# Small-number chains of a graph attention moved to GpSimd, its row work held behind the pairs, and its sums centred by the product that turns them

## The chip, the core and the metric

The kernel runs on one core of a Trainium2 chip. The core has five engines that work side by side: TensorE (PE) for matrix products, VectorE (DVE) and ScalarE (ACT) for elementwise work, GpSimd (POOL)[...], and SyncE (SP), which here only issues loads. Each engine runs its own instructions in a fixed order and waits for others at semaphores. Data lies in SBUF (128 partitions); matrix products land in PSUM[...]. The metric is the device time of one execution in microseconds (us), lower is better.

## The reference

Four layers of a graph network act on 4096 nodes of 64 features, with one dense 4096 x 4096 matrix of 0/1 edges `adj`. Each ends in a residual sum and a LayerNorm.

```python
x = _layernorm(x + _L0_gnn_ref(x, adj, L0_gnn_W, L0_gnn_b))     # mean over neighbours, linear, relu
x = _layernorm(x + _L1_gnn_ref(x, adj, L1_gnn_r, ...))          # hyperbolic attention
x = _layernorm(x + _L2_gnn_ref(x, adj, L2_gnn_weight, ...))     # weights that decay along the neighbours
x = _layernorm(x + _L3_gnn_ref(x, adj, L3_gnn_att_w, ...))      # hyperbolic attention
```

The change concerns the two attentions, which compute the same thing with small differences:

```python
adj_att = jax.nn.sigmoid(left[:, None] + right[None, :] + b_att[0]) * adj   # 4096 x 4096
x_local = logmap(x[:, None, :], x[None, :, :], c)                           # 4096 x 4096 x 64
support_t = jnp.einsum('ij,ijd->id', adj_att, x_local)
return proj(expmap(x, support_t, c), c)
```

The pairwise part (first three lines) is the large one. What follows, `expmap` and `proj` with the residual sum and the LayerNorm, works row by row: for each node a few dot products over its 64 features, then some eighty operations on single numbers (square roots, a tanh, quotients), and at the end the new row as a combination of the old row and `support_t`.

## The kernel before

Nodes are cut into 32 blocks of 128 and, as the receiving side, into four groups of 1024 (eight blocks each; `GROUPS`, taken from the last to the first; this text numbers them 0 to 3 in the order in which they run). The four layers follow each other: layer 0 (stage 0), the first attention (stage 1), the decaying layer (stage 2), the second attention (stage 3). The array `place` holds the stage and a counter of places in it.

**Pairs.** In an attention, `attend` (L914) goes over the 32 source blocks of a group, two at a time: 16 pairs per group. For each block PE forms `z` (128 x 1024, six products: L935, L938, L941), ACT makes the sigmoid (L943) and a square (L946), DVE joins z with the sigmoid (L949). Then DVE finishes both blocks at once (L951, inputs `sq` and `t`, both in SBUF), and PE adds them up in `acc` (L955). At the end of a group ACT copies `acc` to `sums` (L962), features along the partitions.

**Row work.** `move` (L972) is what follows the sums of a group: four transposes bring them to rows (`to_rows_of`, L969), ACT copies them to SBUF (L985), DVE takes the sum over the features (L988), subtracts the mean (L991); POOL multiplies by x (L992), ACT squares (L994), DVE reduces both (`uu` L997, `d` L999). Then comes the chain of small numbers on DVE, each instruction on 128 x 8 elements (one number per node): L1001 to L1065, with three reciprocal square roots of ten instructions each (`rsqrt`, L673 to L679: an integer seed and three Newton steps), a tanh on ACT (L1020) and a reciprocal (L1036). At the end POOL multiplies x by `p` (L1067), DVE multiplies u by `q` (L1068) and adds both (L1071). `norm_rows`, `prepare`, `linear` and `spread_left` are other row work: they make the next layer's inputs.

**What sets the order.** Row work is written as generators. `tick` (L592) is called between the pairs; at each place it lets the generators of two queues go one step, and `yield n` asks for n places until the next. `later` puts a generator into one of the queues; a queue works off one generator after the other. `after`, `soon` and `near` choose the n. But these places only set the order in which the program is written: in the attentions a scheduler of the framework orders each engine's instructions by its own estimate of what is ready, so that an instruction of row work can be issued earlier or later than where it was written (in stages 0 and 2 PE and ACT are held in the written order). At the end of each group `attention` (L1266) queues `move` of that group and, from the second group on, what turns the previous group's result into the next layer's input (`behind`: `linear` in the first attention, the output DMA in the second). Both go into the first queue, except in the last group.

## Time and profile before

| | us |
|---|---|
| median of 3 runs (1148.69 to 1153.72) | 1151.56 |
| the profiled execution | 1150.32 |
| its span (first to last instruction) | 1148.8 |
| layer 0 until the first pair of the first attention | 192.23 |
| first attention, first to last pair | 192.23 to 535.98 |
| second attention, first to last pair | 779.12 to 1111.37 |
| last pair to the last row operation | 1111.37 to 1142.82 |
| one L949 / L951 on DVE (mean) | 1.216 / 2.289 |
| one small instruction on DVE (128 x 8) | 0.16 |
| one large row operation on DVE (128 x 512) | 0.68 |
| one large product on POOL (L992, 128 x 512) | 1.28 |

The profile comes from one execution. Its busy column gives each engine's busy time; a row of the groups tells line, engine, operation, tiles, count, busy time and mean duration. An instruction's duration includes a part in which the next one already runs: on DVE, starts of neighbours are about 0.08 us closer than the durations suggest. Of an attention's groups each has a first L949 and a last L951; the time between them is what the group takes. An idle time carries the name of the engine that ended it.

### The profile page before, as it was taken

How to read it: one execution, taken by the hardware profiler on the slowest of the kernel's cores; microseconds unless marked ns; L12 is line 12 of the kernel's file. 1: busy time of each engine (PE TensorE's matmuls, PEld its weight loads, DVE VectorE, ACT ScalarE, POOL GpSimd, SP SyncE). 2: the span in 40 equal slices, each digit the busy share in tenths (PEclk: the TensorE clock that was granted, in tenths of full speed). 3: DMA queues.
4: the chain of work that ended last, by engine and by line, in shares of the span. 5: the costliest groups of instructions: out<-in, count | busy, mean ns of one | idle time of the engine just before them, and what ended most of it. 6: DMA issues, size and time to landing. Idle time of an engine off the chain costs nothing.

```text
span 1148.8 us, 13484 instructions
## 1 busy us (share of the span) xinstructions
PE 1012.6 (88%) x4832; PEld 386.9 (34%) x4917; DVE 964.3 (84%) x1901; ACT 820.6 (71%) x886; POOL 60.3 (5%) x97
## 2 busy tenths in 40 slices
PE   6999897899899999988999987898898999999870
PEld 3445544233333333332333232233333333233320
DVE  5687898999999899989773476529998999999996
ACT  0003215899889788976767778888998998889850
POOL 0020120000000000000000020000000000000001
PEclk9999998999999999999999999899999999999995
DMA  9999998556566466644988976686465666566400
GB/s 344 421 381 400 373 417 329 193 176 218 176 210 218 164 209 210 220 169 140 323 297 312 341 268 235 220 278 235 150 217 183 220 218 204 204 210 206 149 1 21
DMA packets 38418, 271.57 MB, mean 236 GB/s; under 512 B 4550, under 2 KB 4550, under 8 KB 5574
## 3 DMA queue, kind: packets, MB, share of 16 engines
q1 hardware_dynamic: 37440, 269.50, 65.3%
q10 hardware_dynamic: 902, 1.12, 0.3%
q8 instruction: 40, 0.66, 0.2%
q14 instruction: 36, 0.29, 0.1%
HBM read 269.55 MB, written 1.05 MB: 236 GB/s over the span
## 4 chain that ended last, share of the span: by engine, by line
DVE 57%; PE 26%; ACT 7%; DMA 4%; issue 3%; POOL 2%; SPq 0%; ACTq 0%; POOLq 0%
DVE t L951 20%; DVE t L949 20%; PE z L1372 8%; PE acc L1387 5%; PE acc L955 4%; DMA edges<-in_adj_dram 4%; PE acc L1229 3%; DVE junk L741 2%; ACT sq L946 2%; ACT sq L1381 2%; PE z L935 1%; PE z L938 1%; POOL sq L768 1%; PE aux L842 1%; PE z L941 1%
## 5 line engine op out<-in xcount | busy, mean ns | idle before, releaser
L943 ACT ACTIVATE sig<-left_b,right 128x1024 f32<-128x1024 f32 x256 | 293.8, 1149 | 45.9 <-DVE t L949 35.0
L949 DVE SCALAR_TENSOR_TENSOR t<-z,sig 128x1024 f32<-128x1024 f32 x256 | 309.9, 1216 | 13.9 <-ACT sq L946 12.9
L946 ACT ACTIVATE sq<-z,turn 128x1024 f32<-128x1024 f32 x256 | 281.5, 1106 | 27.3 <-PE z L941 25.1
L951 DVE SCALAR_TENSOR_TENSOR t<-sq,t 128x2048 f32<-128x2048 f32 x128 | 292.9, 2289 | 0.7
L955 PE MATMUL acc<-t,xe 128*64 128x512 f32 x1024 | 260.2, 619 | 32.3 <-DVE t L951 28.7
L935 PE MATMUL z<-edges,two_i 128*128 128x512 bf16 x465 | 183.1, 394 | 19.7 <-DVE t L949 19.5
L938 PE MATMUL z<-lo_hi,hi_lo 128*128 128x512 f16 x512 | 194.1, 379 | 3.2
L941 PE MATMUL z<-dst,src 74*128 74x512 f16 x512 | 195.1, 381 | 0.0
L1381 ACT ACTIVATE sq<-z,at_edge 128x512 bf16<-128x512 f32 (+1 forms) x192 | 152.6, 829 | 51.3 <-PE z L1372 47.9
L955 PEld LDWEIGHTS acc<-t,xe 128*64 128x64 f32 x1024 | 64.0, 138 | 168.5 <-DVE t L951 88.4
L741 DVE SCALAR_TENSOR_TENSOR t<-edges 128x2048 bf16<-128x2048 f32 x32 | 73.9, 2311 | 38.5 <-DMA edges<-in_adj_dram 37.5
L1372 PE MATMUL z<-edges,pass_by 128*128 128x512 bf16 x241 | 87.5, 400 | 17.3 <-ACT sq L1381 15.8
L935 PEld LDWEIGHTS <-two_i 128*128 128x128 bf16 x512 | 50.3, 98 | 142.7 <-issue 97.7
L1229 PE MATMUL acc<-edges,first 128*128 128x512 bf16 x241 | 77.4, 397 | 21.4 <-DMA edges<-in_adj_dram 20.7
L1387 PE MATMUL acc<-sq,halves 128*64 128x512 bf16 x512 | 82.0, 398 | 5.7 <-ACT sq L1381 3.5
L1372 PE MATMUL z<-edges,enter 128*128 128x512 bf16 x240 | 85.1, 397 | 0.1
L1229 PE MATMUL acc<-edges,third 128*65 128x512 bf16 x256 | 80.9, 398 | 0.6
L741 DVE SCALAR_TENSOR_TENSOR junk<-edges 128x2048 bf16<-128x2048 f32 x32 | 73.2, 2286 | 5.1 <-DMA edges<-in_adj_dram 4.8
L938 PEld LDWEIGHTS <-hi_lo 128*128 128x128 f16 x512 | 50.3, 98 | 67.9 <-issue 23.7
L941 PEld LDWEIGHTS <-src 74*128 74x128 f16 x512 | 49.4, 96 | 69.2 <-issue 4.0
L1229 PEld LDWEIGHTS <-first 128*128 128x128 bf16 x256 | 24.3, 98 | 50.2 <-issue 22.6
L1387 PEld LDWEIGHTS <-halves 128*64 128x64 f16 x512 | 18.9, 108 | 63.0 <-issue 62.7
(260 smaller groups left out, 758.3 us busy)
## 6 DMA issues: line engine op xcount, KB each, us to landing
edges<-in_adj_dram SPq DMA_DIRECT2D x256, 1024.0 KB, 4.9
x<-in_x_dram SPq DMA_DIRECT2D x4, 256.0 KB
out_dram<-x ACTq DMA_DIRECT2D x4, 256.0 KB, 4.0
w_sb<-in_L_gnn_W_dram ACTq DMA_DIRECT2D x1, 32.0 KB, 4.8
given<-in_L_gnn_b_dram ACTq DMA_DIRECT2D x1, 0.2 KB
given<-in_L_gnn_bias_dram ACTq DMA_DIRECT2D x1, 0.2 KB
given<-in_L_gnn_b_att_dram ACTq DMA_DIRECT2D x1, 0.0 KB
given<-in_L_gnn_att_b_dram ACTq DMA_DIRECT2D x1, 0.0 KB
```

The lines of the kernel that those rows point to most:

```text
L741: V.scalar_tensor_tensor(junk, a, 0.0, a, ALU.not_equal, ALU.not_equal, accum_out=odd[:, n : n + 1])
L935: nc.tensor.matmul(half, two_i, edge[:, at : at + W], start=True, stop=False)
L938: nc.tensor.matmul(half, hi_lo[:, of], lo_hi[:, to], start=False, stop=False)
L941: nc.tensor.matmul(half, src[:, of], dst[:, to], start=False, stop=True)
L943: nc.scalar.activation(sig, left_b, AF.Sigmoid, bias=right[:, j : j + 1])
L946: nc.scalar.activation(sq[:, k], zp, AF.Square, bias=turn, scale=-1.0 / UNIT)
L949: V.scalar_tensor_tensor(t[:, k], zp, 0.0, sig, ALU.max, ALU.mult)
L951: V.scalar_tensor_tensor(t, sq, HIGH**2, t, ALU.add, ALU.mult)
L955: nc.tensor.matmul(acc[h * D : (h + 1) * D, :], xe[:, j, :], t[:, k, h * W : (h + 1) * W], start=j == BLOCKS[0], stop=j == BLOCKS[-1],)
L1229: nc.tensor.matmul(accs[h][:m], lhs[:, j, :], edge[:, at : at + W], start=j == BLOCKS[0], stop=j == BLOCKS[-1],)
L1372: nc.tensor.matmul(z[:, h : h + W], lhs, rhs[:, h : h + W], start=j == BLOCKS[0], stop=True, skip_group_check=True,)
L1381: nc.scalar.activation(w, z[:, :n], AF.Exp, bias=at_edge, scale=-LN2)
```

## The change

It has five parts.

1. A class `Small` carries the chain of small numbers in `move`. For all groups of an attention but the last it issues them on POOL, for the last on DVE as before. On POOL a fused operation (two in one) becomes two instructions (`stt`). The three integer seeds of the reciprocal square roots and the one reciprocal stay on DVE. The last three large operations also go to POOL (L1067, L1068, L1071 of before).
2. `pool_done` gives the number of places that the writing order leaves for POOL's work before an instruction of another engine that needs it.
3. The four transposes of `sums` become four products with a constant `centre` (128 x 130), which give the rows with their mean taken off and, as a 65th column, their sum. They come in two parts, each with its own ACT copy; L988, L989 and L991 go.
4. The reciprocal of `un` (L1018) becomes two small operations on the reciprocal square root, with two constants from `curved`.
5. `mark` records, at each place, the last instruction of the pairs on PE, ACT and DVE, and ties every row instruction of these engines that is issued there behind it in the engine's order (without a semaphore). This holds in groups 1 to 3 of an attention. The work `behind` now goes to the second queue in all groups, after nine places.

```diff
+            ROW_ENGINES = FIXED | {mybir.EngineType.DVE}
...
+            def mark(rows):
+                traced = nc.cur_bb.bb.instructions
+                for i in traced[seen[0] :]:
+                    if i.engine not in ROW_ENGINES:
+                        continue
+                    if not rows:
+                        pairs_last[i.engine] = i
+                    elif anchored[0] and i.engine in pairs_last:
+                        tc.add_manual_dep(
+                            i, pairs_last[i.engine].name,
+                            mybir.DependencyInfo(
+                                mybir.DependencyClass.NoSync, mybir.DependencyReason.DATA
+                            ),
+                            reason="row work behind the pairs",
+                        )
+                seen[0] = len(traced)
...
             def tick(n):
                 for _ in range(n):
                     place[1] += 1
+                    mark(False)
                     for queue in queues:
...
+                    mark(True)
...
+            def pool_done(small, large=0):
+
+                return 2 + int(small * 0.2 + large * 0.9)
...
+            class Small:
+                def __init__(self, on_pool):
+                    self.on_pool = on_pool
+                    eng = nc.gpsimd if on_pool else V
...
+                def stt(self, out, in0, scalar, in1, op0, op1):
+                    if not self.on_pool:
+                        V.scalar_tensor_tensor(out, in0, scalar, in1, op0, op1)
+                        return
+                    t = nums("pool_t")
+                    nc.gpsimd.tensor_scalar(t, in0, scalar, None, op0)
+                    nc.gpsimd.tensor_tensor(out, t, in1, op1)
+
+                def wait(self, small, large=0):
+
+                    return pool_done(small, large) if self.on_pool else soon()
+
+                def rsqrt(self, a, name, small):
+
+                    r, t = nums(name), nums("rs_t")
+                    if self.on_pool:
+                        yield self.wait(small)
+                    V.tensor_scalar(
+                        r.bitcast(I32), a.bitcast(I32), -0.5, float(0x5F3759DF),
+                        ALU.mult, ALU.add,
+                    )
+                    for _ in range(3):
+                        self.mul(t, r, r)
+                        if self.on_pool:
+                            self.mul(t, t, a)
+                            self.ts(t, t, -0.5, 1.5, ALU.mult, ALU.add)
+                            self.mul(r, t, r)
+                        else:
+                            self.stt(t, t, -0.5, a, ALU.mult, ALU.mult)
+                            self.stt(r, t, 1.5, r, ALU.add, ALU.mult)
+                    return r
...
+            centre = keep.tile([P, 2, D + 1], F32, name="centre")
+            V.memset(centre, 0.0)
+            for h in range(2):
+                of = slice(h * D, (h + 1) * D)
+                V.tensor_scalar(
+                    centre[of, h, :D], ident[of, of], -1.0 / D, None, ALU.add
+                )
+                V.memset(centre[of, h, D:], 1.0)
...
-                t = to_rows_of(sums)
-                yield near()
-                nc.scalar.copy(of.rearrange("p (h k) f -> p h k f", h=2), t)
-                held.pop()
-                yield near()
-                V.tensor_reduce(sum_1, of, AX.X, ALU.add)
-                V.tensor_scalar(k, sum_1, 1.0 / D, None, ALU.mult)
-                yield soon()
-                V.tensor_sub(u, of, over(k))
+                all_u = row.tile([P, WB, D + 1], F32, name="u_1")
+                u, sum_1 = all_u[:, :, :D], all_u[:, :, D]
+                for part in range(2):
+                    yield from free()
+                    t = take(F32, P, 2, 2, D + 1)
+                    for i in range(2):
+                        cols = slice((2 * part + i) * P, (2 * part + i + 1) * P)
+                        nc.tensor.matmul(t[:, i], sums[:, cols], centre, start=True, stop=True)
+                    yield near()
+                    nc.scalar.copy(
+                        all_u.rearrange("p (h k) f -> p k h f", h=2)[:, 2 * part : 2 * part + 2], t
+                    )
+                    held.pop()
+                    yield near()
                 nc.gpsimd.tensor_mul(w, xg, u)
-                yield after(12)
                 nc.scalar.activation(sq, u, AF.Square)
...
+                G = Small(s != GROUPS[-1])
+                yield G.wait(0, 1) if G.on_pool else near()
                 V.tensor_reduce(uu, sq, AX.X, ALU.add)
                 yield soon()
                 V.tensor_reduce(d, w, AX.X, ALU.add)
                 yield soon()
-                V.scalar_tensor_tensor(k, d, c2, sum_1, ALU.mult, ALU.add)
-                V.tensor_mul(k, k, rb[:, at])
+                yield soon()
+                G.stt(k, d, c2, sum_1, ALU.mult, ALU.add)
+                G.mul(k, k, rb[:, at])
...
-                V.reciprocal(r_un, un)
-                yield after(29)
+                G.ts(r_un, r, by_root, 1.0 / fac, ALU.mult, ALU.mult)
+                G.ts(r_un, r_un, by_short, None, ALU.min)
+                yield pool_done(19) if G.on_pool else after(29)
                 nc.scalar.activation(th, un, AF.Tanh, scale=lam)
...
+                if G.on_pool:
+                    yield G.wait(14)
                 V.reciprocal(den, den)
...
+                E = nc.gpsimd if G.on_pool else V
                 nc.gpsimd.tensor_mul(w, xg, over(p))
-                V.tensor_mul(u, u, over(q))
+                E.tensor_mul(u, u, over(q))
                 yield soon()
                 yield soon()
-                V.tensor_add(x_of(layer + 1)[:, at, :], u, w)
-                yield after(72)
+                E.tensor_add(x_of(layer + 1)[:, at, :], u, w)
+                yield pool_done(15, 3) if G.on_pool else after(72)
...
                     if n:
-                        last = n + 1 == NW
-                        later(in_turn((layer + 1, s + 1), behind(s + 1)), last, 9 * last)
+                        later(in_turn((layer + 1, s + 1), behind(s + 1)), True, 9)
                     later(move_s)
```

## The prediction

> **What bounds the kernel now.** I read the page's busy times and slices first, then the busy time by stretch, one stretch per attention group (a group is 1024 rows: 16 pairs of blocks).
>
> ```profile
> PE 1012.6 (88%) x4832; PEld 386.9 (34%) x4917; DVE 964.3 (84%) x1901; ACT 820.6 (71%) x886; POOL 60.3 (5%) x97
> ...
> DVE  5687898999999899989773476529998999999996
> ```
>
> DVE is at nine tenths through both attentions (slices 7 to 18 and 27 to 38), POOL is free. By group:
>
> ```profile
> core 0: us, PE busy (x) PEld busy (x) DVE busy (x) ACT busy (x) POOL busy (x), PEclk, DMA share, GB/s
> 192.23:278.98 86.75, 78.49 (x354) 28.31 (x359) 83.90 (x117) 79.08 (x78) 3.17 (x8) 0.97 0.56 194
> 278.98:361.91 82.93, 77.61 (x327) 26.77 (x332) 79.83 (x112) 72.75 (x70) 1.28 (x1) 0.98 0.60 203
> 362.13:448.62 86.49, 81.38 (x351) 29.20 (x354) 81.55 (x117) 74.37 (x75) 2.32 (x2) 1.00 0.57 195
> 448.69:535.98 87.29, 79.56 (x342) 28.24 (x348) 83.03 (x111) 73.25 (x71) 2.31 (x2) 0.99 0.57 193
> ...
> 865.93:948.93 83.00, 77.69 (x327) 26.77 (x332) 79.83 (x112) 72.75 (x70) 1.27 (x1) 0.98 0.59 203
> 949.16:1031.52 82.36, 77.40 (x327) 26.59 (x330) 80.93 (x118) 72.31 (x71) 2.32 (x2) 0.98 0.61 208
> 1031.52:1111.37 79.85, 72.43 (x308) 24.76 (x314) 79.85 (x109) 68.23 (x64) 2.32 (x2) 1.00 0.40 135
> ```
>
> The first row is group 0 of the first attention, then come groups 1 to 3 of each attention. Only these six can change; between their first and last instructions they take 257.0 + 245.4 = 502.4 us. Is DVE their bound? DVE's timeline (start, duration, engine, line) in the late pairs of group 0, which have no row work:
>
> ```profile
> 248.24 2.29 DVE L951 SCALAR_TENSOR_TENSOR t<-sq,t 128x2048 f32<-128x2048 f32 x1
> 250.54 2.55 DVE L949 SCALAR_TENSOR_TENSOR t<-z,sig 128x1024 f32<-128x1024 f32 x2
> 253.12 2.29 DVE L951 SCALAR_TENSOR_TENSOR t<-sq,t 128x2048 f32<-128x2048 f32 x1
> ...
> 257.74 2.29 DVE L951 SCALAR_TENSOR_TENSOR t<-sq,t 128x2048 f32<-128x2048 f32 x1
> ```
>
> From 248.24 to 257.74 two pairs take 9.50, so 4.75 each. Late in the second attention one small instruction stands in every gap:
>
> ```profile
> 1090.10 2.29 DVE L951 SCALAR_TENSOR_TENSOR t<-sq,t 128x2048 f32<-128x2048 f32 x1
> 1092.31 0.17 DVE L1009 TENSOR_SCALAR t<-t 128x8 f32<-128x8 f32 x1
> ...
> 1094.84 2.29 DVE L951 SCALAR_TENSOR_TENSOR t<-sq,t 128x2048 f32<-128x2048 f32 x1
> ```
>
> Again 4.74. A small instruction costs about 0.075 (next start after 1092.31: 1092.38), so three fill the 0.25 that DVE has spare per pair, and cost nothing. PE alone needs 4.53 of a pair (1.87 for `acc`, twelve products at 0.222), so 16 x 4.74 = 75.8 us is a group's floor here. The six groups are 47.4 us above it. That is large row work and stalls: in group 1, the pair with both sums and the wait for POOL takes 9.00, and 1.7 follows two pairs later because PE, having idled 1.74 and 1.31 us, runs its next products at half speed:
>
> ```profile
> 292.90 3.53 PE L955 MATMUL acc<-t,xe 128*64 128x512 f32 x8 [1.31 <-DVE t L951]
> ```
>
> against 1.94 elsewhere. Last, the tail: 31.45 us from the last L951 (1111.37) to the last add (1142.82), nearly all a DVE chain. The previous group's row work is still half undone there and goes first; the last group's begins only here:
>
> ```profile
> 1124.26 0.69 DVE L991 TENSOR_TENSOR u<-z,k 128x512 f32<-128x512 f32 x1
> 1126.40 0.69 DVE L999 TENSOR_REDUCE d<-w_att 128x8 f32<-128x512 f32 x1 [1.44 <-POOL w_att L992]
> ```
>
> **What the skill says.** "SBUF — State Buffer", Who interferes with whom: a VectorE instruction with two SBUF inputs and a GpSimd one that reads SBUF exclude each other for a whole instruction, whoever came first; with one SBUF input there is no conflict. The trace agrees, both ways. The timeline at 666 us:
>
> ```profile
> 666.07 2.28 DVE L741 SCALAR_TENSOR_TENSOR t<-edges 128x2048 bf16<-128x2048 f32 x1
> 666.22 2.22 POOL L806 COPY ys<-hl 128x16 f16<-128x16 f16 x1 [0.26 <-DVE hl L803]
> ```
>
> L806 takes 0.22 beside L949 (at 227.78), which reads PSUM and one SBUF tile, but 2.22 here. The other way, L795 took 1.54 instead of 0.68 behind POOL's L768. "GPSIMD Engine Reference", 3.1 Elementwise: about 2.6 cycles per element at 1.2 GHz for two inputs against VectorE's 1, and a dispatch in software; L992 (512 elements) took 1.28, so all but about 0.17 is elements. "TensorE: Matmul & The Clock Gate", Part 1: idle windows of some 3.4 us halve the clock; the 3.53 above fits.
>
> **Part 1: chains to POOL.** 94 POOL instructions per move: 90 small, four large. DVE keeps two reductions and four small ones (three seeds, one reciprocal). The built program places them at: uu and d in pair 2, seed before L951 of pair 4, reciprocal at the head of pair 8, seeds before L951 of pair 9 and at the head of pair 12. Gone from a group are 72 small DVE instructions (mostly hidden, so about nothing), sum_1, u, u x q and the add (four of about 0.60), and the 1.4 wait for POOL.
>
> The new cost: each of the four waits for a POOL chain, and DVE stands with all the pairs behind it. No row shows a dependent small POOL operation. Lower bound: 0.13 to 0.16, the spacing of independent copies (227.78, 227.91, 228.05, 228.21). Upper: 0.22 to 0.25 for one, plus DVE's release of POOL (0.08), with a mean of 0.43 for L811 beside DVE work as the extreme. I take 0.28 per dependent and 0.15 per free step. POOL has only the two L949 of a pair, some 2.3 us, since L951 shuts it out. First stretch, 11 steps in two windows: no wait. Pair 4 to tanh, 15 steps (14 dependent): 4.1 in two windows of 4.6, just in time. After tanh 11 dependent + 3 free = 3.5 in one window: 1.2 left over, done behind L951, so the reciprocal waits 1.3. To pair 9: 3.4 in 4.6, free. To pair 12: 18 x 0.28 + 3 x 0.15 = 5.5 in 4.6: waits 1.0. Sum 2.3 per group; a wait can't be below nothing, so quick steps bring at most these 2.3 back. L951 meeting a POOL instruction in flight waits too: up to 0.25 for small ones, inside DVE's spare 0.25; for the three large at the end (1.04, 1.04, 1.28) I take 0.5.
>
> **Part 2: centring by a product.** Per move four products with 130 columns in place of four transposes, two ACT copies of 260 columns (0.37 each, estimated from 0.58 for 512) in place of one of 512. What stays at the group's head: two reductions 1.2 less DVE's spare 0.25, and ACT's 0.57 + 0.74 + 0.62 = 1.9, which in the kernel before hid under DVE's 4.3; I take 1.8 in all.
>
> **Part 3: order.** `mark` adds no semaphore; it keeps row work of DVE, PE and ACT from going ahead of the pairs. In groups 2 and 3 of the first attention `linear` now lies spread over pairs 4 to 6 of the second queue: ACT 2 x (0.57 + 0.38), DVE 2 x 0.42, PE waiting for ACT's copies; I take 2.5. The `left_b` copies are spread over pairs 12 to 14: nothing, as in group 0 (pair 10, no longer than others). Output DMAs on ACT's queue come at pair 4 of the next group; the last at pair 15 of group 3 waits for POOL's add, which I expect in pair 14. `centre` and the constants are built during the first layer, whose DVE has gaps: nothing.
>
> **Tail.** With the previous move done, the last one starts when acc is ready (1114.71): copy 0.57, products 1.0, second copy 0.4, POOL 1.28, so d starts near 1118.2 instead of 1126.4. From there the same 16.4 chain (last group: still DVE). Gain 8.2.
>
> **Sum.** A group: 75.8 + 1.8 + 0.5 + 2.3 + 0.2 = 80.6; with `linear` 83.1. First attention 80.6 + 2 x 83.1 = 246.8 against 257.0: gain 10.2. Second 3 x 80.6 = 241.8 against 245.4: 3.6. Tail 8.2. Sum 22.0. The profiled execution, 1150.3 (span 1148.8), becomes 1128.3; the median shown, 1151.6, lies 1.2 above it, so 1129.5.
>
> **Rivals.** *DVE is the bound*, by its busy column: 72 x 0.075 + 2.4 + 1.4 = 9.2 per group, six times, and the tail: 63 off, 1088. Against it stands 4.75 in pairs without row work; the floor allows 47.4 + 8.2 = 55.6, 1096. If POOL is quick (0.2 a step, no wait) I get 1129.5 less six times 2.3: 1116. *POOL is late*: at 0.40 a step the chain to tanh needs 5.8 in 4.6, so ACT stands at tanh (about 2.4, the next pairs' sigmoids and squares behind it), the reciprocal waits 1.6, the third seed 3.1, the second 0.2: 7.3; PE's half clock adds 1.7. That is 9.0 instead of 2.3, six times 6.7 = 40 more: 1169, slower. For it stands 0.43 for L811; against it, 0.13 between free copies. It decides from waits of about 6 per group, a step of 0.36. *The row work only changes place*: the groups keep 502.4, since the heads and `linear` cost what they did, and the tail alone gains: 1143. Against it, of the 4.3 us of DVE work and waiting in the 9.00 pair, 2.9 go.
>
> **Chances.** Forecast (waits of 1 to 4 per group) 0.63; quick POOL or DVE rule 0.12; late POOL 0.19, of which 0.13 over 0.5% slower; same groups 0.06, a third within 0.5%. A difference of 0.5%, 5.8 us, is about what a measurement here tells from none. Faster 0.79, same 0.08, slower 0.13. The range runs from 1104 (no waits; heads and `linear` at half their price, six times 0.9 and twice 1.2 less, and a little for the locks) to 1160 (a step of about 0.38); the forecast's own is 1116 to 1140.
>
> **What would show it.** POOL busy some 25 to 35 us per group; DVE waits named POOL at the reciprocal and the third seed, 1 us each; none at the other two; small POOL rows of about 2.2 where L951 runs; pairs of 4.74 between; d of the last group 7 us after the last L951. Wrong if ACT waits for POOL at tanh, or if pairs without row work fall below 4.74.

## The result, and the profile after

The changed kernel takes 1165.2 us in the median of 4 runs (1159.0 to 1166.0); the kernel before, run beside it, 1151.5. The ratio is 1.0104, with a 95% interval of 1.0081 to 1.0127: 1% slower, where 1129.5 was predicted. The profiled execution took 1165.4, its span (first to last instruction) 1163.6.

The page after, engine totals and DVE's slices:

```profile
PE 1025.5 (88%) x4949; PEld 392.5 (34%) x4949; DVE 917.2 (79%) x1450; ACT 822.9 (71%) x894; POOL 279.0 (24%) x649
...
DVE  6587888988988798899563476519898988888975
```

DVE lost 47 us of work and some 450 instructions, POOL has 219 us more (blocked time included), and the kernel is slower. By stretch (first L1032 to last L1034 of groups 1 to 3 of each attention, and last the tail; L1032 is L949 of before, L1034 is L951, L1029 the square L946):

```profile
279.31:365.12 85.81, 78.59 (x337) 27.27 (x336) 75.65 (x56) 72.86 (x72) 38.68 (x94) 0.98 0.58 196
365.04:454.97 89.93, 80.13 (x360) 29.79 (x360) 76.46 (x58) 74.77 (x76) 38.64 (x94) 1.00 0.55 187
454.89:544.67 89.78, 79.22 (x352) 28.64 (x352) 79.28 (x60) 74.11 (x73) 40.75 (x94) 1.00 0.56 187
...
876.19:960.62 84.43, 76.90 (x337) 27.01 (x336) 75.83 (x56) 72.85 (x72) 40.57 (x94) 1.00 0.59 199
960.54:1048.02 87.48, 80.00 (x336) 27.63 (x336) 75.67 (x56) 72.94 (x72) 38.64 (x94) 0.96 0.58 196
1047.94:1137.03 89.09, 77.69 (x318) 25.94 (x318) 76.03 (x58) 68.81 (x66) 36.45 (x94) 0.94 0.37 124
1137.03:1163.60 26.57, 3.37 (x17) 1.53 (x17) 13.95 (x82) 2.18 (x5) 2.73 (x2) 0.61 0.04 14
```

The six groups, 501.9 us before by this measure, take 526.5: 24.6 lost. In each, DVE is busy about 4 to 5 us less than before and the group is longer. The tail from the last L1034 to the end of the span falls from 37.4 to 26.6: 10.8 gained. The groups that the change doesn't touch (group 0) are 1.3 and 1.4 us longer; they lie between 86.8 and 89.4 in the runs below without a pattern.

So DVE waits. For whom? Waits over the whole span, with engine and line that waited, releaser, then total, times and longest; first the one line of the kernel before, then lines of the changed one:

```profile
DVE t L949 <- ACT sq L946: 12.9, 7, 2.4
```

```profile
DVE t L1032 <- ACT sq L1029: 62.6, 38, 4.7
...
ACT th L1113 <- POOL un L1107: 8.1, 6, 1.8
...
ACT sq L1029 <- POOL x L1168: 4.9, 1, 4.9
...
DVE d L1087 <- POOL w_att L1080: 1.8, 2, 1.1
```

Before, DVE waited 12.9 us for the square and now 62.6. Of POOL it hardly sees anything: 1.8 us, after the last groups, and no wait at the reciprocal or at a seed. But ACT stands for POOL in two places, at the tanh and ahead of a square, and DVE stands behind ACT.

**The chain on POOL.** POOL's timeline in group 1, from the first seed to the tanh (start, duration, engine, line), and the L1034 of DVE that its fifth line meets:

```profile
304.79 2.22 POOL L741 TENSOR_TENSOR rs_t<-r_t 128x8 f32<-128x8 f32 x1 [2.54 <-DVE r_t L736]
307.08 0.20 POOL L743 TENSOR_TENSOR rs_t<-rs_t,t 128x8 f32<-128x8 f32 x1
307.37 0.20 POOL L744 TENSOR_SCALAR rs_t<-rs_t 128x8 f32<-128x8 f32 x1
307.65 0.20 POOL L745 TENSOR_TENSOR r_t<-rs_t,r_t 128x8 f32<-128x8 f32 x1
...
309.33 2.29 POOL L743 TENSOR_TENSOR rs_t<-rs_t,t 128x8 f32<-128x8 f32 x1
...
312.84 0.33 POOL L1107 TENSOR_SCALAR un<-un,k_short 128x8 f32<-128x8 f32 x1
```

```profile
309.28 2.29 DVE L1034 SCALAR_TENSOR_TENSOR t<-sq,t 128x2048 f32<-128x2048 f32 x1
```

Dependent steps start 0.28 apart (307.37 less 307.08 is 0.29, 307.65 less 307.37 is 0.28): the step that the prediction took. The first and the fifth line are operations that met L1034, which has two SBUF inputs, and stayed until it ended: they took 2.22 and 2.29 us instead of 0.20, as the Trainium skill says ("SBUF — State Buffer", Who interferes with whom). So POOL was busy 36 to 41 us per group, above the 25 to 35 that were forecast. ACT at the same time:

```profile
308.12 2.31 ACT L1026 ACTIVATE sig<-left_b,right 128x1024 f32<-128x1024 f32 x2
310.40 1.11 ACT L1029 ACTIVATE sq<-z,turn 128x1024 f32<-128x1024 f32 x1
313.20 0.21 ACT L1113 ACTIVATE th<-un 128x8 f32<-128x8 f32 x1 [1.68 <-POOL un L1107]
313.31 1.10 ACT L1029 ACTIVATE sq<-z,turn 128x1024 f32<-128x1024 f32 x1
```

The tanh stands *between* the two squares of a pair. It waits 1.68 for POOL; the second square starts at 313.31 (at 311.76 in the run below in which the tanh stands behind it), and L1032 behind it at 314.44 after 1.67 of idle time. The chain is done in the pair for which it was reckoned, but not at the tanh's place in it. This is one of the two signs of being wrong that the prediction named: ACT waits for POOL at the tanh.

**The pairs.** Starts of L1034 in group 1 are 4.58 to 4.88 apart (4.72 in the mean, as in the late pairs of group 0 before and after; 4.74 was predicted), except 7.65 and 5.66 at the head, 6.43 at the tanh, and 7.05 and 6.99 at the two `left_b` copies (`left_b` is the sigmoid's input for the next group, which ACT copies to SBUF in two halves). In groups 2 and 3 of the first attention `linear` adds two pairs of 8.88 and 9.10, and the last group of the second attention has one of 9.44.

The pair of 6.99 has a second cause. PE's timeline ahead of it:

```profile
337.00 1.94 PE L1038 MATMUL acc<-t,xe 128*64 128x512 f32 x8
...
341.72 0.39 PE L1018 MATMUL z<-edges,two_i 128*128 128x512 bf16 x1 [1.14 <-DVE t L1032]
...
344.04 3.63 PE L1038 MATMUL acc<-t,xe 128*64 128x512 f32 x8 [0.84 <-DVE t L1034]
```

The same eight products take 3.63 instead of 1.94 once, at a granted clock of 0.53 (344.00 to 347.60; 1.00 in the 4 us before and behind), and 1.69 is what this pair has above the 5.30 of the same pair in group 1 of the second attention. In group 2 there it happens twice (3.62 and 3.44 us; pairs of 6.58 and 6.80). The three cost 4.9 us; two more stand in the last group (3.51 and 3.46). They come after short waits of PE for DVE, but after the same waits, 1.14 and 0.85, the set at 396.79 took 1.94 at 1.00: what decides it isn't shown.

### The profile page after: what moved, and what is told of

Its sections match the earlier page's. It is cut to its first block, busy times and chain, and to the rows that moved or that the text cites. A ratio compares the mean times of both kernels' runs of the same rounds, so it can differ in the third digit from the quotient of the medians.

```text
span 1163.6 us, 13739 instructions
## 1 busy us (share of the span) xinstructions
PE 1025.5 (88%) x4949; PEld 392.5 (34%) x4949; DVE 917.2 (79%) x1450; ACT 822.9 (71%) x894; POOL 279.0 (24%) x649
## 4 chain that ended last, share of the span: by engine, by line
PE 42%; DVE 32%; ACT 12%; DMA 6%; POOL 5%; issue 2%; ACTq 0%; SPq 0%; POOLq 0%
DVE t L1034 13%; DVE t L1032 11%; PE z L1470 9%; PE acc L1038 9%; ACT sq L1029 5%; PE acc L1485 5%; DMA edges<-in_adj_dram 5%; PE z L1018 4%; PE acc L1326 3%; PE z L1024 3%; PE z L1021 3%; ACT sig L1026 2%; DVE junk L820 1%; ACT sq L1479 1%; POOL rs_t L743 1%
## 5 line engine op out<-in xcount | busy, mean ns | idle before, releaser
L1032 DVE SCALAR_TENSOR_TENSOR t<-z,sig 128x1024 f32<-128x1024 f32 x256 | 308.2, 1219 | 65.7 <-ACT sq L1029 62.6
L1029 ACT ACTIVATE sq<-z,turn 128x1024 f32<-128x1024 f32 x256 | 282.8, 1108 | 30.9 <-PE z L1024 23.6
L1034 DVE SCALAR_TENSOR_TENSOR t<-sq,t 128x2048 f32<-128x2048 f32 x128 | 294.4, 2300 | 3.1
L1018 PE MATMUL z<-edges,two_i 128*128 128x512 bf16 x512 | 202.0, 394 | 36.4 <-DVE t L1032 34.9
L1326 PE MATMUL acc<-edges,first 128*128 128x512 bf16 x256 | 80.3, 395 | 22.6 <-DMA edges<-in_adj_dram 22.4
L1018 PEld LDWEIGHTS <-two_i 128*128 128x128 bf16 x512 | 50.4, 98 | 131.1 <-issue 83.0
L1470 PE MATMUL z<-edges,enter 128*128 128x512 bf16 x256 | 90.8, 396 | 0.0
L1080 POOL TENSOR_TENSOR w_att<-x,u 128x512 f32<-128x512 f32 x8 | 9.4, 1180 | 246.1 <-ACT u L1075 246.1
L851 POOL TENSOR_TENSOR sq<-z 128x512 f32<-128x512 f32 x8 | 14.2, 1777 | 191.3 <-DVE z L850 181.5
```

The lines of the kernel that those rows point to most:

```text
L1018: nc.tensor.matmul(half, two_i, edge[:, at : at + W], start=True, stop=False)
L1029: nc.scalar.activation(sq[:, k], zp, AF.Square, bias=turn, scale=-1.0 / UNIT)
L1032: V.scalar_tensor_tensor(t[:, k], zp, 0.0, sig, ALU.max, ALU.mult)
L1034: V.scalar_tensor_tensor(t, sq, HIGH**2, t, ALU.add, ALU.mult)
L1326: nc.tensor.matmul(accs[h][:m], lhs[:, j, :], edge[:, at : at + W], start=j == BLOCKS[0], stop=j == BLOCKS[-1],)
L1470: nc.tensor.matmul(z[:, h : h + W], lhs, rhs[:, h : h + W], start=j == BLOCKS[0], stop=True, skip_group_check=True,)
```

## The experiments

Each is the changed kernel with the edit shown, unless it says otherwise. In all of them the kernel before lies at 1151.9 to 1152.8; ratios are to it.

| run | median us | ratio (95%) |
|---|---|---|
| no_pin | 1207.8 | 1.0486 (1.0461 to 1.0511) |
| queue_back | 1167.5 | 1.0142 (1.0105 to 1.0178) |
| before_pin | 1152.5 | 1.0002 (0.9987 to 1.0018) |
| small_dve | 1143.9 | 0.9932 (0.9907 to 0.9958) |
| before_centre | 1142.5 | 0.9904 (0.9876 to 0.9933) |
| cut_both | 1158.2 | 1.0043 (1.0025 to 1.0061) |
| tanh_late1 | 1152.2 | 0.9998 (0.9973 to 1.0023) |
| ggqq_f_late1 | 1155.8 | 1.0029 (1.0015 to 1.0042) |
| tail_tied | 1150.4 | 0.9969 (0.9952 to 0.9986) |
| lin_all_dve | 1146.7 | 0.9960 (0.9945 to 0.9975) |
| dve_lin | 1145.6 | 0.9949 (0.9930 to 0.9968) |
| lin_pe | 1147.0 | 0.9946 (0.9921 to 0.9972) |
| lin_none | 1136.9 | 0.9866 (0.9848 to 0.9883) |
| mix | 1145.5 | 0.9933 (0.9911 to 0.9954) |
| half | 1138.4 | 0.9862 (0.9841 to 0.9884) |

### Which part of the change costs the time?

My first theory (A) was that the ties hold ACT's and PE's row work at bad places. Four runs, one part of the change each.

```diff
# no_pin
-                    anchored[0] = n > 0
+                    anchored[0] = False
```

> The changed kernel with `anchored` never true: the row work is not tied behind the pairs, all else stays. Changed kernel 1165.2, kernel before 1151.5. The six groups lost about 25 us and the tail gained 10.8. Theory A (the ties hold ACT's and PE's row work at fixed places among the pairs, and what stands behind it is late): most of the loss goes, 1138 to 1145, and DVE's waits for the square (62.6 us at L1032) fall to 15 to 25. Theory B (the tanh on ACT waits for POOL, 8.1 us in all, and the squares behind it): nothing of it goes, 1160 to 1166. Theory C (the second queue puts `linear` and the output among the move): 1158 to 1165. Theory D (the sums turned in two parts cost more at the head): 1160 to 1165.

```diff
# queue_back
-                        later(in_turn((layer + 1, s + 1), behind(s + 1)), True, 9)
+                        last = n + 1 == NW
+                        later(in_turn((layer + 1, s + 1), behind(s + 1)), last, 9 * last)
```

> The changed kernel with the work `behind` in the first queue again, except in the last group, as before. Theory C: the two groups with `linear` lose their 4.1 and 4.3 us at pairs 4 and 6, and the last group its 4.7 at pair 13: 16 to 21 us less, 1144 to 1150. Theory A: the work is tied at another place and costs there what it cost: 1158 to 1170. Theories B and D: within 5 us of 1165.

```diff
# small_dve
-                G = Small(s != GROUPS[-1])
+                G = Small(False)
```

> The changed kernel with the chains of small numbers on DVE in all groups (as its last group has them), with all else kept. Theory B: the tanh no longer waits for POOL, and its pair loses its 1.8 us six times; with what stands behind it 8 to 11 us less, 1154 to 1157. Theory A: POOL is not what costs; the chains on DVE add the 1.4 us wait and about 2.4 us of large work per group, partly in DVE's spare time: 1163 to 1180. Theories C and D: 1160 to 1175.

```diff
# before_pin: the kernel before, with `mark` as in the change, and
                     place[1] += 1
+                    mark(False)
                     for queue in queues:
...
+                    mark(True)
...
                         need((layer, s, "left"))
+                    anchored[0] = n > 0
```

> The kernel before with nothing but `mark` (the ties) added, in groups 1 to 3 of each attention. Theory A: the ties alone make it slower, 1165 to 1180 (the loss of 25 us, without the 10.8 of the tail). Theories B, C and D: within 5 us of 1151.5.

Theory A falls, twice: the ties alone change nothing in the time (before_pin), and without them the changed kernel is 43 us slower still, which none of the four theories forecast. DVE's timeline of no_pin in group 1 shows why:

```profile
289.27 2.28 DVE L1034 SCALAR_TENSOR_TENSOR t<-sq,t 128x2048 f32<-128x2048 f32 x1
296.70 0.20 DVE L1131 RECIPROCAL den<-den 128x8 f32<-128x8 f32 x1 [5.15 <-POOL den L1128]
...
299.40 0.17 DVE L736 TENSOR_SCALAR n<-mt 128x8 int32<-128x8 int32 x1 [1.40 <-POOL mt L1145]
...
307.12 0.17 DVE L736 TENSOR_SCALAR n<-w 128x8 int32<-128x8 int32 x1 [3.09 <-POOL w L1158]
```

Free to move them, the scheduler issues the reciprocal and the seeds earlier, and DVE stands 5.15, 1.40 and 3.09 us; over the six groups these three come to 31.6, 5.9 and 14.8, and ACT waits 26.9 at the tanh instead of 8.1. The ties are what keeps these waits out of the changed kernel. The queue (C) makes no difference in sum, but it does in place: in the profile of queue_back the two groups with `linear` are 3.6 longer each (93.5 and 93.4), the last two of the second attention 7.9 and 4.2 shorter (79.6 and 84.9), where the tanh now stands behind both squares of its pair and waits 0.71; stage 2 and the tail take the gain back (4.3 and 1.8). And with the chains back on DVE the kernel is 21 us faster than the changed one and faster than before: the loss belongs to the chains on POOL as they are placed here (B), though B expected only 8 to 11 of it.

### Does the centring pay?

The kernel before, with the rows by `centre` and without the sum and the subtraction on DVE; nothing else.

```diff
# before_centre: the kernel before, and
-                t = to_rows_of(sums)
+                for part in range(2):
...
+                        nc.tensor.matmul(t[:, i], sums[:, cols], centre, start=True, stop=True)
...
-                V.tensor_reduce(sum_1, of, AX.X, ALU.add)
-                V.tensor_scalar(k, sum_1, 1.0 / D, None, ALU.mult)
-                V.tensor_sub(u, of, over(k))
```

> The kernel before with the sums centred by the product in two parts (part 3 of the change), and nothing else. Its own sum of the prediction: the pair with 9.00 falls by about 1.3 and the wait for POOL of 1.4 goes, six times, and the tail's DVE work falls by about 1.4: 1140 to 1146. Theory D (the two copies and the products at half the clock cost as much as they save): 1149 to 1156.

It does, by 10 us (D falls), but hardly in the groups. They take 81.25, 86.40, 87.20 and 81.24, 81.12, 83.48, in sum 500.7 against 501.9. The tail takes 29.6 instead of 37.4. With nothing of POOL's chains, ties or queue, this is as fast as small_dve (1143.9), whose six groups are 6.6 shorter in the profile and whose tail is 3.3 longer: over the whole, ties and queue bring nothing to it.

### How does POOL make it slower?

```diff
# cut_both
-                        r.bitcast(I32), a.bitcast(I32), -0.5, float(0x5F3759DF),
+                        r.bitcast(I32), (self.still if self.on_pool else a).bitcast(I32), -0.5, float(0x5F3759DF),
...
-                nc.scalar.activation(th, un, AF.Tanh, scale=lam)
+                nc.scalar.activation(th, x2g if G.on_pool else un, AF.Tanh, scale=lam)
...
-                V.reciprocal(den, den)
+                V.reciprocal(den_r, x2g if G.on_pool else den)
```

> The changed kernel with all of POOL's work kept, but no engine waiting for the chain in the first part of it: the three seeds and the reciprocal on DVE and the tanh on ACT read `x2` instead of POOL's numbers (so the numbers that follow are not the reference's). ACT's issue order stays that of the changed kernel. Theory E1 (what costs is the waiting for POOL at the tanh): the tanh's pair loses its 1.8 us and the rest stays or gains a little, 1150 to 1158. Theory E2 (what costs is ACT's order from the tanh on, set by where the tanh is written: the left_b pairs keep 7.05 and 7.0): 1154 to 1163, with the left_b pairs unchanged. Theory F (POOL's instructions slow DVE and the others by being there): 1160 to 1167.

```diff
# tanh_late1
-                yield pool_done(19) if G.on_pool else after(29)
+                yield pool_done(19) + 1 if G.on_pool else after(29)
```

> The changed kernel with the tanh written one place later. In the built program it then stands behind both squares of its pair (with two sigmoids next) instead of between them, and the `left_b` copies behind it fall back into the order of the kernel with the chains on DVE, except in groups 2 and 3 of the first attention, where the tanh still stands behind one square. Theory E2: the tanh's pair falls from 6.43 to about 4.8 in four groups, and the two left_b pairs from 14.0 to about 10.5 in the four groups that have them: 4 x 1.6 + 4 x 3.5 = 20 us less, 1142 to 1149. Theory E1: only the tanh's wait goes, 1155 to 1160. Theory F: 1162 to 1168.

ggqq_f_late1 has the later tanh too, issues both sigmoids of a pair ahead in the text, and adds this tie:

```diff
# ggqq_f_late1
+                        tc.add_manual_dep(squared.ins, sig_last.ins.name, ..., reason="both sigmoids ahead")
```

> The tanh one place later as in the run beside it, and each pair's first square tied behind its second sigmoid in ACT's order, so that the two sigmoids go ahead everywhere. Theory E2: the regular order saves what is left of it at the head and around `linear`: 0 to 8 us less than with the later tanh alone, 1136 to 1147. Rival: a square held back by a sigmoid that waits for its buffer makes DVE late: 2 to 10 us more than with the later tanh alone.

Without any waiting for the chain, 7 us return (cut_both); the pair at the tanh falls from 6.43 to 4.86 and that at the first `left_b` copy stays at 7.05. Moving the tanh by one place returns 13: 1152.2 lies between the forecasts of E1 and E2, and cut_both's 1158.2 in both, but for 0.2. ACT's timeline of tanh_late1, at the tanh and at the `left_b` copy:

```profile
310.44 1.12 ACT L1029 ACTIVATE sq<-z,turn 128x1024 f32<-128x1024 f32 x1
311.76 1.11 ACT L1029 ACTIVATE sq<-z,turn 128x1024 f32<-128x1024 f32 x1 [0.21 <-PE z L1024]
313.24 0.21 ACT L1113 ACTIVATE th<-un 128x8 f32<-128x8 f32 x1 [0.36 <-POOL un L1107]
313.36 2.17 ACT L1026 ACTIVATE sig<-left_b,right 128x1024 f32<-128x1024 f32 x2
...
335.94 1.11 ACT L1029 ACTIVATE sq<-z,turn 128x1024 f32<-128x1024 f32 x1 [0.64 <-PE z L1024]
336.95 0.58 ACT L993 COPY left_b<-aux 128x512 f32<-128x512 f32 x1
337.42 2.19 ACT L1026 ACTIVATE sig<-left_b,right 128x1024 f32<-128x1024 f32 x2
```

The tanh is executed at the same time as before (313.2), but both squares are ahead of it. And the order behind it is another: two sigmoids, two squares, the copy behind both squares. In the changed kernel ACT's timeline at the same `left_b` copy is:

```profile
335.71 1.09 ACT L1029 ACTIVATE sq<-z,turn 128x1024 f32<-128x1024 f32 x1
338.11 1.15 ACT L1026 ACTIVATE sig<-left_b,right 128x1024 f32<-128x1024 f32 x1 [1.31 <-DVE t L1032]
339.30 1.11 ACT L1029 ACTIVATE sq<-z,turn 128x1024 f32<-128x1024 f32 x1
340.31 0.58 ACT L993 COPY left_b<-aux 128x512 f32<-128x512 f32 x1
340.77 1.13 ACT L1029 ACTIVATE sq<-z,turn 128x1024 f32<-128x1024 f32 x1
```

Here one sigmoid of the pair stands behind a square, waits 1.31 for DVE to release a buffer, and makes the next square late. With that gone the pair goes from 7.05 to 5.22. So both halves of E are there: E1 the wait, E2 the order. (The three sets of products at 3.4 to 3.6 us, 4.9 in all, are gone from these pairs too.) The groups without `linear` or that last wait fall to 81.2, 81.3 and 81.3. Forcing the two sigmoids ahead everywhere saves nothing more: the six groups take 511.5 against 512.2. Its 1155.8 is on the rival's side, but the two intervals overlap, and the profile has the difference outside these groups. F isn't needed: cut_both, with all of POOL's work but no waits, lies 7 below the changed kernel, and groups without `linear` take the same with POOL's chains as without (dve_lin, below).

### The output DMA

The last group still took 89.3. ACT's timeline there, in the changed kernel:

```profile
1115.04 1.09 ACT L1029 ACTIVATE sq<-z,turn 128x1024 f32<-128x1024 f32 x1
1120.63 0.34 ACTq L1505 DMA_DIRECT2D out_dram<-x  x1
1121.02 1.11 ACT L1029 ACTIVATE sq<-z,turn 128x1024 f32<-128x1024 f32 x1 [4.88 <-POOL x L1168]
```

ACT doesn't issue the output DMA before POOL's add is done (1119.42 plus 1.18), and the squares wait behind the DMA. That DMA is written after the last pair, where `anchored` is already false, so that it is not tied and was issued among the pairs.

```diff
# tail_tied: tanh_late1, and
-                anchored[0] = False
+                anchored[0] = layer == 3
```

> The tanh one place later (as before: 1152.2), and the ties kept on after the last pair, so that the output DMA written there can't be issued among the last group's pairs. In the built program it moves behind the last group's copy of `acc`. If the 6.3 us for which ACT stood at that DMA for POOL's add were on the path: pair 13 of the last group falls from 10.85 to about 4.8 and the time by 5 to 7 us, 1145 to 1147. Rival: the add is late anyway and the stand moves into the tail, so that the tail grows by 2 to 6 us: 1148 to 1153.

The last group falls from 89.27 to 83.05, by 6.2, and pair 13 from 10.85 to 4.79. Of this the median shows 1.7 only, and 1150.4 lies in the rival's range: the tail is 28.9 in this profile instead of 26.6, as the rival said, and stage 2, which the edit doesn't touch, differs by 4. The gain in the group is shown; how much of it the whole keeps isn't settled by these runs.

### `linear`

Groups 2 and 3 of the first attention still take 89.7 and 89.8, with `linear` in them.

```diff
# lin_all_dve: tail_tied, and
-                    nc.scalar.copy(xt, t[:D])
+                    (V.tensor_copy if layer == 2 else nc.scalar.copy)(xt, t[:D])
...
-                nc.scalar.activation(halves[:, at, :D], t, AF.Copy, scale=SUP)
+                V.tensor_scalar(halves[:, at, :D], t, SUP, None, ALU.mult)
```

> As the run beside it, and in the first attention `linear` makes both of its ACT copies (`x_t` and the first half of `halves`) on DVE instead, so that ACT's order stays two sigmoids, two squares. If the 8 us over the other groups in groups 2 and 3 come from ACT's order broken by those copies (pairs of 8.6 and 9.1): the two groups fall from 88.8 and 90.4 to 83 to 84, 11 to 13 us less than the run beside it, 1132 to 1136. Rival: PE's own products of `linear` (0.6 and 1.1 us ahead of the pair's products) are what costs, or DVE's extra 2 us a group take it back: 0 to 6 us less, 1140 to 1147.

dve_lin is the same with `Small(False)`.

> The same with all small numbers on DVE (POOL as in the kernel before). If POOL's chain frees nothing that the pairs need, its groups come out as with POOL, 81 to 84, and only the tail is longer by some 6 us, since the chain of the group before the last is still running there: 1138 to 1143. If DVE's time bounds the groups after all, they are longer by 72 x 0.075 = 5.4 us each: 1160 or more.

Two further runs take `linear` away from these two groups, all of it (lin_none) or all but PE's products (lin_pe).

```diff
# lin_none: tail_tied, and
-            attention(1, curve1, (2, 1, 1, 1), lambda s: linear(2, s, w2_sb, supports))
+            attention(
+                1, curve1, (2, 1, 1, 1),
+                lambda s: left_out(s) if s in GROUPS[:2] else linear(2, s, w2_sb, supports),
+            )
# left_out: nothing in lin_none; in lin_pe the transposes of x and these products
+                        nc.tensor.matmul(
+                            t[:, k, :], still[:, k * P : (k + 1) * P], w2_sb, start=True, stop=True
+                        )
```

> As the kernel with the later tanh and the ties kept on after the last pair (1150.4; its groups 2 and 3 of the first attention take 89.7 and 89.8), with `linear` left out in these two groups (its result is filled with a constant once, so the numbers that follow are not the reference's). Both theories: what `linear` costs in all. If it is the 8.5 us over the other groups: the two groups fall to 81 to 82, 1131 to 1136. If other row work of these groups costs part of it: 83 to 87 each, 1137 to 1146.

> The same, with only PE's share of `linear` kept (the transposes and the products, the products from a constant), and no copy and no other consumer (numbers not the reference's). If the hops from PE to ACT or DVE and back in four in-order queues cost the 8.5: groups of 82 to 84 and 1133 to 1140. If PE's products alone cost it, by pushing the pair's products late (3.4 us of PE work a group, about what PE has spare in 16 pairs): groups of 86 to 90 and 1143 to 1151.

ACT's copies are not it: with them on DVE the groups take 88.5 and 90.4. Without `linear` they take 81.2 and 82.8, and the kernel 13.5 us less. With PE's products alone they take 88.2 and 91.4. PE's timeline of lin_pe:

```profile
380.22 1.03 PE L1038 MATMUL acc<-t,xe 128*64 128x512 f32 x4
381.18 0.63 PE L1393 MATMUL aux<-ident,x 128*64 128x128 f32 x4
381.73 1.10 PE L1402 MATMUL aux<-w_sb,still 64*128 64x64 f32 x8
382.77 0.40 PE L1018 MATMUL z<-edges,two_i 128*128 128x512 bf16 x1
...
384.10 0.60 PE L1393 MATMUL aux<-ident,x 128*64 128x128 f32 x4
```

and DVE's at the same time:

```profile
381.56 2.29 DVE L1034 SCALAR_TENSOR_TENSOR t<-sq,t 128x2048 f32<-128x2048 f32 x1
385.45 1.23 DVE L1032 SCALAR_TENSOR_TENSOR t<-z,sig 128x1024 f32<-128x1024 f32 x1 [1.60 <-ACT sq L1029]
389.18 1.23 DVE L1032 SCALAR_TENSOR_TENSOR t<-z,sig 128x1024 f32<-128x1024 f32 x1 [2.51 <-ACT sq L1029]
...
390.44 2.29 DVE L1034 SCALAR_TENSOR_TENSOR t<-sq,t 128x2048 f32<-128x2048 f32 x1
```

Row products of 0.6 and 1.1 us stand in PE's order ahead of the pair's z, the square comes late, DVE stands 1.60 and 2.51, and L1034 starts 8.88 after the last one: the same 8.88 as with all of `linear`. ACT's order is broken here too (sigmoid and square alternate), so that product and order can't be told apart by this run. What is shown is that neither copies nor hops between engines are needed for the loss. PE's own time can't be all of it: in small_dve the same products stand closer together, three of the four within 392.38 to 396.52, and the group takes 83.9 against 80.5 in the second attention, 3.4 more, which is their own time. (The other group with `linear` takes 83.1 there; groups without it 80.5 to 82.3.) Why they cost twice as much behind POOL's chains stays open.

dve_lin shows what POOL's chains are worth with tanh and output DMA mended: 1145.6 against 1146.7, no difference, where 1138 to 1143 was expected. Its groups without `linear` (82.1, 82.1, 80.5, 82.3) come out as those with POOL (81.1, 81.3, 81.3, 83.1), and the tail is longer (33.1 against 28.6), as expected. But its two groups with `linear` take 84.5 and 87.1 against 88.5 and 90.4: POOL's chains lose 7.3 us there and win 4.5 in the tail.

### A version that beats both

```diff
# half: tail_tied, and
-                G = Small(s != GROUPS[-1])
+                G = Small(layer == 3 and s != GROUPS[-1])
```

> A kernel meant to beat both: POOL carries the small numbers in the second attention only (but for its last group), the first attention keeps them on DVE; the tanh one place later and the ties kept on after the last pair. If the parts add up: first attention as with the chains on DVE (82.2, 83.9, 83.1), second as with the ties kept on (81.3, 81.3, 83.0), tail 27 to 29 instead of 33: 1137 to 1141. If they don't: 1143 to 1150.

mix keeps POOL for one group only: `Small(layer == 3 and s == GROUPS[-2])`.

> The same with POOL only for the last but one group of the second attention. Groups as with the chains on DVE, tail 27 to 29 if POOL's chain ends before the last pair does: 1136 to 1141; if it ends later, because the chain before it on DVE is longer and holds it up, 1141 to 1148.

It takes each side where that was better: DVE in the attention with `linear`, POOL ahead of the tail. half comes out at 1138.4, inside what the sum of the parts gave: 1.4% under before and 2.3% under the changed kernel. Against before_centre (0.9904) its interval just overlaps. Its groups are the expected ones to 0.2, but for one of 83.2; its tail is 30.1 in the profile, where 27 to 29 was expected. mix is slower: its last group takes 91.9. There the chain of the group ahead ends late on DVE, POOL's starts late, and DVE's reciprocal comes in the pair behind the first seed's. DVE's timeline of mix:

```profile
1076.73 2.29 DVE L1034 SCALAR_TENSOR_TENSOR t<-sq,t 128x2048 f32<-128x2048 f32 x1
1086.06 0.20 DVE L1131 RECIPROCAL den<-den 128x8 f32<-128x8 f32 x1 [7.04 <-POOL den L1128]
```

## Why the prediction was wrong

**The floor** was right. Pairs without row work stay at 4.72 to 4.75 in the mean, with or without small operations on DVE, and 5 us less DVE work in a group bring nothing. The rival that took DVE's busy column for the bound is refuted, also by dve_lin.

**Part 1, the step that failed: "Pair 4 to tanh, 15 steps (14 dependent): 4.1 in two windows of 4.6, just in time".** The step of 0.28 is right, the windows are right. But "in time" was reckoned to the end of a window on DVE, and the one who waits is ACT, whose tanh stands in the middle of a pair between two squares. It was late by 1.68 there (8.1 in six groups), and the pair was longer by as much. The waits that were priced, 1.3 at the reciprocal and 1.0 at the third seed, didn't come, and don't come in tanh_late1 either, where ACT waits for 1.8 in all: the reciprocal has two windows behind the tanh, not the one that I gave it (POOL ends at 318.98, the reciprocal starts at 322.50). The rival "POOL is late" had this mechanism (ACT stands at the tanh) and forecast 1169; but it tied it to a step of 0.36, and it needs none beyond 0.28, since the place decides. That its number lies near the measured one is chance: its waits at the reciprocal and the seeds aren't there.

**Part 3, "The `left_b` copies are spread over pairs 12 to 14: nothing".** In the changed kernel the first costs 2.3 to 2.5 (pairs of 7.05 to 7.22) and the second 0.6, because from the tanh on ACT's order is no longer two sigmoids, two squares; where the second pair takes 6.99 and 6.80, the rest is the slow products of PE (1.7 and 1.5). With the tanh one place later each costs 0.5. I compared them with those of group 0, which are issued in another order. Wait, order and the slow products behind them together are 14.3 us of the six groups (526.5 to 512.2 with the later tanh).

**Part 3, the output DMA.** I saw the wait ("the last at pair 15 of group 3 waits for POOL's add, which I expect in pair 14") and gave it no price. It cost 6.2: ACT stood 4.9, and the pairs behind it.

**Part 3, "`linear` ... I take 2.5"** was mis-sized: 8.5 in group 2 (89.7 less 81.2; 1.5 of it is one slow set of products, in a pair of 10.61) and 7.0 in group 3 (89.8 less 82.8). The sum had ACT's and DVE's instructions and left out PE's own products, twice 0.6 and 1.1 us, 3.4 in all, which PE has to spare only over all 16 pairs (0.2 in each); in two pairs they don't fit. That is their own time; the rest, as much again, comes with the order in which they stand, and its cause stays open. Against 5.0 priced, 10.5 more.

**Two readings** of the prediction were off. L806, at 227.78, ended 0.08 us into L949; L807 and L809 behind it, 0.22 each, are the copies that ran beside it. And the 3.53 of PE came after idle times of 1.74 and 1.31: half speed is there (a granted clock of 0.54), an idle time of 3.4 us isn't.

**Ties.** "`mark` adds no semaphore" and costs nothing: right (before_pin). I didn't see what they are for: without them the chain on POOL is waited for everywhere.

**Part 2** was right in its sum, not in its place: centring alone gains 10, and the groups gain 1.2 of it. At the head I took 1.8; three pairs there take 7.65, 5.66 and 4.58, 3.7 above 14.2. The sum for a group, 80.6, is near the 81.2 of the mended kernels, since the waits of 2.3 that aren't there about cover it.

**Tail.** 8.2 forecast, 10.8 measured; d of the last group starts 5.6 us after the last L1034 ends (forecast: 7). But the forecast put this down to the chain on POOL, and centring alone, with both chains on DVE, brings 7.8 of it (before_centre: d 8.5 after, instead of 15.0). That 8.2 is near 7.8 is chance; with the centring in both, POOL's chains are worth 4.5 in the tail (dve_lin).

**The balance.** Forecast 488.6 for the six groups, measured 526.5, 37.9 more: tanh and order 14.3, `linear` 10.5, output DMA 6.2, together 31.0. The other 6.9 are found in the mended kernel without `linear` too: its six groups take 490.8, 7.2 above 6 x 80.6, two thirds of it in the last pair of group 3 (6.98, where the next layer begins; 6.99 before) and in the last group (83.1). The tail gives 2.6 back. These are differences of single profiles; groups in the same order mostly agree within 0.1 us between runs, and where they don't, a slow set of products is in one of them. (The forecast's sum for a group has 0.2 for which it names no step.)

## What to carry to other kernels

When a chain moves to another engine, reckon when it must be done at the place that its consumer has in its own engine's order, not by the end of a window: an instruction that waits for 1.7 us between two squares delays all that follows, while one place later it waits 0.36 and no square stands behind it. Price every instruction that waits on an engine's queue, DMA issues too, and moved products on the engine that runs them against what that engine has to spare in that very pair. And where the small operations are hidden already, as a steady pair of unchanged length shows, moving them buys nothing: here it paid in the tail alone (4.5 us), where nothing is left to hide them, and cost more than that in the groups with `linear`.

## What was not expected of the hardware

On POOL, dependent operations on 128 x 8 elements, tensor with tensor or with a constant, start 0.28 to 0.32 us apart and independent ones 0.16 (L1133 and L1134: 322.78 and 322.94). Those that take a number per partition from SBUF last longer, 0.27 to 0.33 instead of 0.20 to 0.24. One that begins as little as 0.05 us after an L1034 of DVE (309.33 and 309.28) stays for all of it, 2.2 to 2.3, so that a dependent chain stands for a whole L1034 in each pair. On the other side L1034 is hardly slower for it: 2.300 in the mean with POOL's chains, 2.289 before.
